# A four-layer graph network on one core: rows of indirect transfers, the place of the first keys, the last block of a scan, and the tables of the attention layer

## The chip, the cores and the metric

The kernel runs on one core of a Trainium2 chip. Its time is the time of one execution on the device in microseconds (us); a version is judged by the median over several executions. One further execution is recorded by the hardware profiler and gives the page and the trace that are read here. A core has five engines with a queue of instructions each: TensorE (PE, its weight loads are listed as PEld), VectorE (DVE), ScalarE (ACT), GpSimd (POOL) and SyncE (SP). SP, ACT and POOL also issue DMA transfers.

## The reference

There are 6250 nodes with 16 features each and 200000 edges sorted by their target node. Every layer gathers a row per edge by `src`, and reduces the rows of each target node `dst`.

```python
m = jnp.tanh(x[src] * edge_weight[:, None])                      # layer 0
agg0 = jax.ops.segment_sum(m, dst, num_segments=x.shape[0])
# layer 1, per edge a 16x16 matrix of messages and one of logits
e1 = (efeat @ W_msg + b_msg).reshape(E, 16, -1) * feat[src][:, :, None]
e2 = (efeat @ W_attn + b_attn).reshape(E, 16, -1) * feat[src][:, :, None]
seg_max = jax.ops.segment_max(e2, dst, num_segments=N)
ex = jnp.exp(e2 - seg_max[dst])
denom = jax.ops.segment_sum(ex, dst, num_segments=N)
agg1 = jax.ops.segment_sum(e1 * ex / denom[dst], dst, num_segments=N).sum(axis=1)
# layer 2
agg2 = jax.ops.segment_max(x[src] * timestamp, dst, num_segments=N) @ W.T + b
# layer 3, twice, relu between the passes
h = (1.0 + eps) * x + jax.ops.segment_sum(x[src], dst, num_segments=n)
h = jax.nn.relu(h @ wa + ba) @ wb + bb
# log_softmax at the end; after every layer
x = _layernorm(x + agg)
```

## The kernel before

**Layout.** 125 partitions hold 50 nodes each, and 1600 consecutive edges each. The edges of a partition are cut into 8 blocks of 200 columns (`NB`, `JB`).

**One scan over the edges.** `edge_scan` (L465) runs for layer 0 ("l0"), for layer 2 ("l2") and for both passes of layer 3 ("l3a", "l3b"). It works under an order written out by hand, and fills for each block a tile `xb` of 200 columns with the rows of the source nodes, from two sides. 120 columns (`NPE`) come from TensorE: ten batches of 12 columns (`BC`), three selects of 4 columns in each. A batch needs one-hot matrices, which DVE makes (L462) of keys loaded from a DRAM tensor `key_d` (L456, two batches ahead); a select is a row of matmuls (L491) of the one-hots with the node features split in three bfloat16 parts, then a DVE multiply that keeps what belongs to the column (L495) and a DVE sum (L500) into `xb`. The other 80 columns are gathered by POOL, one indirect DMA of 125 rows for a column (L97), all 80 issued at the start of a block; `xb` has two buffers. In the third batch of the next block `message` is applied to the whole block (layer 0: multiply by the edge weight L890 and tanh L891; layer 2: multiply; layer 3: nothing), and then 16 scans along the 200 columns, one for each feature (L513 for the maximum, L517 for the sum), go between the selects of that block. Their result goes to a DRAM table of rows. For the last block there is no next one: its message and its 16 scans come after its last select and its last gather.

**From rows to nodes.** After the scan the ends of partitions are carried over, and `at_nodes` (L587) gathers for each of the 50 node columns the row at which the node's edges end, 50 indirect DMAs of 128 rows (tile `an_y`). The 50 columns are taken in two chunks, `CHUNKS = ((0, 40), (40, NJ))`; for each chunk `finish` does the layer's matmuls, the layer normalisation, the store of the new node table (`into_table`) and the split in parts (`split_table`). The order of these two chunks on the engines is decided by the scheduler of the framework.

**The beginning.** `src` and `dst` are loaded, DVE checks whether the edges are sorted (`n_back`), and all engines branch on that (L232, the body sorts). Three large DRAM copies (`ew_d` twice and `ef_d`, 14.4 MB) are issued by ACT before the branch (L220), after a one-element copy `arrived` of `src`. The keys of the first block are made after the branch on DVE and PE (`keys_made`, `keys_turned`, `keys_kept`, up to tile `kT`), stored to `key_d` by SP (L274), and loaded by `edge_scan`. SP's queue after the branch is: the load of `ew` (L887, 800 KB), the store of `key_d`, three loads of keys.

**Beside layer 0.** `prelude` hands `edge_scan` a list of jobs by select number, which prepare layer 1: the search for the last edge of each node, with 51 gathers of 128 rows into `in_run` (`ends_gather`, L406); the list of attention chunks, written by 50 scatters of 128 rows (`chunks_put`, L744); and the edge table `edges_d`. On POOL the `in_run` gathers stand between the gathers of blocks 1 and 2, and the scatters between those of blocks 3 and 4. Tiles `run_i`, `ck_rows` and `ck_at` have 128 partitions, of which the last three are filled with constants.

**Layer 1.** `steps` (L990) makes 220 steps. Each ends with one store of 128 rows of 3 KB (L1083): sums of weights, weighted sums, and maxima, 256 numbers of each. Afterwards one gather `fx` (128 rows) and 50 gathers `r` (128 rows of 3 KB, five into a buffer, three buffers) fetch what the nodes need; ACT takes the logarithm and the exponential of the sums (L1233, L1234), DVE multiplies and sums (L1236, L1237), and the two chunks are finished as above. Of `r` only the first two thirds of a row are used.

Of the kernel before, what the change touches and what calls it, by code (L numbers as in the profile page):

```python
# [41 lines left out]
CHUNKS = ((0, 40), (40, NJ))  # L42
# [5 lines left out]
def tile_gnn_resnorm(ctx: ExitStack, tc: tile.TileContext, a: dict, out: bass.AP):  # L48
# [166 lines left out]
    arrived = consts.tile([1, 1], F32, name="arrived")  # L215
    with tc.manual_schedule():

        nc.scalar.copy(arrived, src[:1, :1])
        for to, of in given[2:]:
            nc.scalar.dma_start(to.rearrange("(p j) f -> p (j f)", p=80),  # L220
                                of.rearrange("(p j) f -> p (j f)", p=80))
    with tc.tile_pool(name="sort", bufs=1) as sp, tc.tile_pool(name="sortp", bufs=1, space=PSUM) as pp:
        back = sp.tile([P, J], F32, name="backwards")
        worst = sp.tile([P, 1], F32, name="worst")
        nc.vector.tensor_tensor(back, dst[:, 1:J + 1], dst[:, :J], op=OP.is_lt)
        nc.vector.tensor_reduce(worst, back, AX.X, OP.max)
        n_ps = pp.tile([1, 1], F32, name="n_ps")
        nc.tensor.matmul(n_ps, worst, ones, start=True, stop=True)
        n_back = sp.tile([1, 1], I32, name="n_back")
        nc.vector.tensor_copy(n_back, n_ps)  # L230
        unordered = nc.values_load(n_back, min_val=0, max_val=P)
        with tc.If(unordered > 0):  # L232
            sort_edges(sp, pp, dst)
            nc.sync.dma_start(src, src_d.rearrange("(p j) o -> p (j o)", j=J))
            load_dst(dst, dst_d.rearrange("e o -> (e o)"))

# [42 lines left out]
    with tc.tile_pool(name="keys0p", bufs=1, space=PSUM) as pp:  # L279
        keys_kept(kp, 0, keys_turned(lambda r, c: pp.tile([128, 512], F32, name="scratch")[:r, :c], keys_made(kp, 0)))  # L280
# [74 lines left out]
    def ends_begin(sp):  # L355
        e = Ends()
        e.runs = sp.tile([P, NR + 1], F32, name="runs")
        nc.vector.tensor_copy(e.runs[:, :NR], dst[:, 1:J + 1].rearrange("p (r k) -> p r k", k=RUN)[:, :, RUN - 1])
        nc.vector.tensor_copy(e.runs[:, NR:], rank[:P])
        edge = sp.tile([P, 2], F32, name="dst_edge")  # L360
        nc.vector.tensor_copy(edge[:, 0:1], dst[:, :1])
        nc.vector.tensor_scalar(edge[:, 1:2], rank[:P], float(P - 1), BIG, op0=OP.is_equal, op1=OP.mult)
        nc.vector.tensor_add(edge[:, 1:2], edge[:, 1:2], e.runs[:, NR - 1:NR])

        e.from_ = sp.tile([P, 2, NJ1], F32, name="from_edge")
        nc.vector.tensor_tensor(e.from_, edge.unsqueeze(2).to_broadcast([P, 2, NJ1]),
                                io[:P, :NJ1].unsqueeze(1).to_broadcast([P, 2, NJ1]), op=OP.subtract)
        nc.vector.tensor_scalar(e.from_, e.from_, 1.0, None, op0=OP.add)
        e.run = sp.tile([P, NJ1], F32, name="run")
        e.run_i = sp.tile([128, NJ1], I32, name="run_i")  # L370
        nc.vector.memset(e.run_i[96:], 0)
        e.inside, e.row_ps = {}, {}
        return e
# [18 lines left out]
    def ends_runs(sp, e, j0):  # L392
# [11 lines left out]
        nc.vector.tensor_copy(e.run_i[:P, here], e.run[:, here])  # L404

    def ends_gather(sp, e):  # L406
        e.in_run = sp.tile([128, NJ1, RUN], I32, name="in_run")
        for j in range(NJ1):
            gather(e.in_run[:, j, :], runs_d, e.run_i[:, j:j + 1])

    def ends_upto(sp, e, j0):
        here = slice(j0, j0 + 17)
        less = sp.tile([P, 17, RUN], BF16, name="less_in")
        nc.vector.tensor_tensor(less, e.in_run[:P, here], nodes[:, here].unsqueeze(2).to_broadcast([P, 17, RUN]),
                                op=OP.is_le)
        nc.vector.tensor_reduce(upto[:, here], less, AX.X, OP.add)
# [37 lines left out]
    def load_keys(ep, k, bufs=2):  # L454
        keys = ep.tile([P, BW], U16, name="keys", bufs=bufs)
        nc.sync.dma_start(keys, key_d[k * BC * P:k * BC * P + BW].partition_broadcast(P))  # L456
        return keys

# [6 lines left out]
    def edge_scan(tag, table, parts, F, message, pen, tmp, beside=None, first=None):  # L465
# [10 lines left out]
        with tc.tile_pool(name=f"es_{tag}", bufs=3) as ep, \  # L476
# [4 lines left out]
            NBT = NPE // BC  # L481
            batches = [(b, c) for b in range(NB) for c in range(NBT)]

# [18 lines left out]
            def scans(xb, b, prev):  # L502
# [3 lines left out]
                if prev is not None:  # L506
                    last = ep.tile([P, F], F32, name="last", bufs=2)
                    nc.vector.tensor_copy(last, prev[:, JB - 1, :])

                def one(f):  # L510
                    if is_max:
                        init = -BIG if last is None else last[:, f:f + 1]
                        nc.vector.tensor_tensor_scan(sc[:, :, f], pen[:, b * JB:(b + 1) * JB], xb[:, :, f],  # L513
                                                     init, op0=OP.add, op1=OP.max)
                    else:
                        init = 0.0 if last is None else last[:, f:f + 1]
                        nc.vector.tensor_tensor_scan(sc[:, :, f], keep[:, b * JB:(b + 1) * JB], xb[:, :, f],  # L517
                                                     init, op0=OP.mult, op1=OP.add)

                pieces = [lambda f=f: one(f) for f in range(F)]  # L520
                pieces.append(lambda: store(nc.sync, rows_v[:, b * JB:(b + 1) * JB, :], sc))
                return sc, pieces

            keys = [load_keys(ep, k) for k in range(0 if first is None else 1, 2)]
            ohs = one_hot(ep, keys.pop(0)) if first is None else first
            prev, todo, waiting = None, [], []
            for k, (b, c) in enumerate(batches):
# [10 lines left out]
                if c == 2 and waiting:  # L538
                    xw, bw = waiting.pop(0)
                    message(xw, bw)  # L540
                    prev, todo = scans(xw, bw, prev)
# [12 lines left out]
            for xw, bw in waiting:  # L554
                message(xw, bw)
                prev, todo = scans(xw, bw, prev)
                while todo:
                    todo.pop(0)()
# [150 lines left out]
    def chunks_set(tmp, num, stop, off_ps, all_ps):  # L709
# [16 lines left out]
        rows_all = tmp.tile([128, NJ, 4], F32, name="ck_rows")  # L726
        nc.vector.memset(rows_all[96:], 0.0)
        rows = rows_all[:P]
# [7 lines left out]
        at = tmp.tile([128, NJ], I32, name="ck_at")  # L736
        nc.vector.memset(at[96:], 128 * Q)
        nc.vector.tensor_copy(at[:P], first)
# [3 lines left out]
        return rows_all, at  # L742

    def chunks_put(rows_all, at):  # L744
        for j in range(NJ):
            nc.gpsimd.indirect_dma_start(
                out=chunk_d[j % NC], out_offset=bass.IndirectOffsetOnAxis(ap=at[:, j:j + 1], axis=0),
                in_=rows_all[:, j, :], in_offset=None, bounds_check=128 * Q - 1, oob_is_err=False)
# [138 lines left out]
    nc.sync.dma_start(ew, ew_d.rearrange("(p j) o -> p (j o)", j=J))  # L887

    def tanh_message(xb, b):
        nc.vector.tensor_mul(xb, xb, ew[:, b * JB:(b + 1) * JB].unsqueeze(2).to_broadcast([P, JB, D]))  # L890
        nc.scalar.activation(xb, xb, AF.Tanh)  # L891

    def prelude(kp):
# [65 lines left out]
        at(10, lambda: put(r=edge_rows_begin(now["rp"])))  # L959
        for i in range(J // WE):  # L960
            for step in range(4):
                at(16 + 3 * i + step, lambda i=i, step=step: edge_rows(now["r"], i * WE, step))
# [6 lines left out]
    rows, carry = edge_scan("l0", a["x"], parts, D, tanh_message, None, lp0, prelude(kp))  # L969
# [15 lines left out]
    rows1 = dram.tile([128 * Q, RW], F32, name="rows_l1")  # L985
    rows1_v = rows1.rearrange("(p t) c -> p t c", t=Q)
    l1o = ctx.enter_context(ExitStack())
    tail = l1o.enter_context(tc.tile_pool(name="l1o", bufs=1)).tile([128, RW], F32, name="tail")
    with tc.tile_pool(name="l1c", bufs=1) as cp:
        def steps(lo, hi, state, between=None):  # L990


            with tc.tile_pool(name=f"l1i{lo}", bufs=3) as ip, \
# [87 lines left out]
                def keep_state(t, ps, st):  # L1081
                    nc.scalar.copy(st[:, :2 * DD], ps)
                    nc.sync.dma_start(rows1_v[:, t, :], st)  # L1083
# [48 lines left out]
        nc.sync.dma_start(rows1_v[:, QS:, :], zero.unsqueeze(1).to_broadcast([128, Q - QS, RW]))  # L1132
# [7 lines left out]
    first = one_hot(fp, load_keys(fp, 0, 1), 1)  # L1140
# [4 lines left out]
    with tc.tile_pool(name="l1t", bufs=1) as lp, tc.tile_pool(name="l1tp", bufs=1, space=PSUM) as pp:  # L1145
# [49 lines left out]
        gather(fx, rows1, fix_row)  # L1195
# [28 lines left out]
        for j0, j1 in CHUNKS:  # L1224
            n = j1 - j0
            y = lp.tile([P, n, D], F32, name=f"y1_{j0}")
            for j in range(j0, j1, GN):
                r = lp.tile([128, GN, RW], F32, name="r", bufs=3)
                for i in range(GN):
                    gather(r[:, i, :], rows1, idx_row_all[:, j + i:j + i + 1])  # L1230
                v = r[:P, :, :2 * DD].rearrange("p j (i k o) -> p j i k o", k=2, o=D)
# [3 lines left out]
                for i in range(GN):  # L1235
                    nc.vector.tensor_mul(A[:, i], A[:, i], L[:, i])  # L1236
                    nc.vector.tensor_reduce(y[:, j - j0 + i, :], A[:, i].rearrange("p i o -> p o i"), AX.X, OP.add)  # L1237
            nc.vector.tensor_mul(y, y, own[:, j0:j1].unsqueeze(2).to_broadcast([P, n, D]))
# [46 lines left out]
    with tc.tile_pool(name="l2", bufs=1) as lp:  # L1285
# [5 lines left out]
        def scaled_message(xb, b):  # L1291
            nc.vector.tensor_mul(xb, xb, ew1[:, b * JB:(b + 1) * JB].unsqueeze(2).to_broadcast([P, JB, D]))

        rows, carry = edge_scan("l2", t2, parts, D, scaled_message, pen, lp, first=first)
        with tc.tile_pool(name="l2p", bufs=2, space=PSUM) as pp:
# [9 lines left out]
            at_nodes(lp, rows, carry, D, True, finish)  # L1305


    def gin(tag, table, parts, xt, F, ws, lp, then):
# [3 lines left out]
        rows, carried = edge_scan(tag, table, parts, F, lambda xb, b: None, None, lp, first=first)  # L1312
        with tc.tile_pool(name=f"{tag}p", bufs=2, space=PSUM) as pp:
# [21 lines left out]
            at_nodes(lp, rows, carried, F, False, finish)  # L1335
# [75 lines left out]
```

## Time and profile before

| what | value |
|---|---|
| median of 6 runs | 7623.91 us (7621.07 to 7626.5) |
| profiled execution | 7624.68 us |
| span of its profile | 7622.9 us |
| granted TensorE clock, mean | 0.957 of full speed |
| PE busy | 6794.4 us, 89% |
| DVE busy | 6744.3 us, 88% |
| POOL busy | 5861.1 us, 77% |
| ACT busy | 1903.4 us, 25% |

Times within the profile are counted from the start of its span. In a row of a timeline the columns are start, duration (of the whole run of `xN` instructions), engine, line, operation, output and inputs, and in brackets the idle time of the engine just before with what ended it. In a row of a group the columns are line, engine, operation, names and count, then busy time and mean duration in ns, then the idle time before them. Layer 0 takes the time up to about 1250 us, layer 1 up to 4324, layer 2 up to about 5440, the passes of layer 3 up to 6529 and to the end.

### The profile page before, as it was taken

To read this page: it belongs to the slowest core of one execution; us is meant where nothing else is said; L and a number is where in the kernel's file an instruction comes from. 1 tells how busy PE (TensorE), PEld (TensorE's weight loads), DVE (VectorE), ACT (ScalarE), POOL (GpSimd) and SP (SyncE) were. 2 spreads that over 40 slices of the span, in tenths; PEclk is the share of its full clock that TensorE was granted. 3 is DMA by queue.
4 is the path that set the end of the run, shared out by engine and by line. 5 is a ranking of instruction groups with operands and counts; after the bars stand their busy time and mean duration, and the time that the engine had idled before them with its cause. 6 is when DMAs were issued, how large, how long until landed. Compare 5 with 4: busy or idle time off the path is not lost. (4 is left out here: it accounts for less than half of the span.)

```text
span 7622.9 us, 133196 instructions
## 1 busy us (share of the span) xinstructions
PE 6794.4 (89%) x55586; PEld 5220.7 (68%) x55586; DVE 6744.3 (88%) x7804; ACT 1903.4 (25%) x3200; POOL 5861.1 (77%) x4906
## 2 busy tenths in 40 slices
PE   5889894999999999999999499998599997899995
PEld 5888894444444444444444399998599997799994
DVE  6999995999999999999999789997588886688985
ACT  0122110555555555555555300000000000000000
POOL 5787886777777777777777588887688887788886
PEclk9999997999999999999999799999799998899997
DMA  4344542122222212222221422222122222122221
GB/s 128 93 115 100 124 95 76 48 53 50 53 50 52 53 50 53 50 53 51 51 53 48 134 45 45 56 46 45 34 47 54 47 54 45 30 53 47 56 45 33
DMA packets 288130, 460.36 MB, mean 60 GB/s; under 512 B 134733, under 2 KB 188133, under 8 KB 283216
## 3 DMA queue, kind: packets, MB, share of 16 engines
q1 hardware_dynamic: 121136, 331.29, 12.8%
q0 software_dynamic: 166032, 105.92, 11.4%
q10 hardware_dynamic: 336, 14.40, 0.6%
q8 instruction: 442, 7.24, 0.4%
q14 instruction: 184, 1.51, 0.1%
HBM read 256.64 MB, written 206.15 MB: 61 GB/s over the span
## 5 line engine op out<-in xcount | busy, mean ns | idle before, releaser
L491 PE MATMUL all_ps<-parts,oh 125*128 125x208 bf16 (+1 forms) x46080 | 4006.8, 251 | 205.8 <-DVE kept L495 78.3
L491 PEld LDWEIGHTS <-oh 125*128 125x128 bf16 x46080 | 3987.4, 99 | 224.8 <-issue 99.3
L97 POOL DMA_INDIRECT hg<-table_x,g x1760 | 2062.2, 1172 | 544.0 <-issue 539.1
L97 POOL DMA_INDIRECT xb<-table_x,src x1280 | 1614.1, 1261 | 434.2 <-issue 414.5
L1077 PE MATMUL la<-e,ident 128*128 128x512 f32 x3520 | 1561.6, 597 | 4.5 <-DVE e L1064 3.8
L500 DVE TENSOR_REDUCE xb<-kept 125x64 f32<-125x832 f32 x960 | 1509.6, 1572 | 33.0
L495 DVE TENSOR_TENSOR kept<-all_ps,place 125x832 f32<-125x832 f32 x960 | 974.4, 1015 | 354.0 <-PE all_ps L491 345.5
L1077 PEld LDWEIGHTS la<-e,ident 128*128 128x128 f32 x3520 | 653.1, 191 | 744.1 <-issue 737.4
L97 POOL DMA_INDIRECT xb<-in_x,src x640 | 834.5, 1304 | 250.8 <-issue 193.9
L1029 DVE TENSOR_TENSOR e<-mm,hg 128x1024 f32<-128x1024 f32 x880 | 1013.5, 1208 | 3.4 <-DMA hg<-table_x,g 3.3
L97 POOL DMA_INDIRECT xb<-table_l3b,src x640 | 796.4, 1244 | 211.4 <-issue 211.4
L1024 PE MATMUL mm<-w_h,eT 98*128 98x512 bf16 x1760 | 668.3, 380 | 236.6 <-DVE e L1029 167.6
L462 DVE TENSOR_SCALAR oh<-keys,mykey 125x1504 bf16<-125x1504 uint16 x1272 | 786.6, 678 | 72.9 <-DMA keys<-key_d 72.9
L1041 ACT ACTIVATE e<-e,epen 128x256 f32<-128x256 f32 x1760 | 797.3, 501 | 113.8 <-DVE e L1029 112.0
L1057 ACT ACTIVATE e<-e 128x1024 f32<-128x1024 f32 x440 | 465.1, 1057 | 1001.7 <-DVE e L1055 984.7
L1025 PE MATMUL mm<-w_l,eT 98*128 98x512 bf16 x1760 | 669.7, 381 | 0.0
L1025 PEld LDWEIGHTS <-eT 98*128 98x128 bf16 x1760 | 169.7, 96 | 636.6 <-issue 532.2
L1055 DVE TENSOR_TENSOR e<-e,st 128x1024 f32<-128x1024 f32 x440 | 519.2, 1221 | 7.7
L1064 DVE TENSOR_TENSOR e<-e 128x1024 f32<-128x1024 f32 x440 | 515.6, 1209 | 0.0
L1024 PEld LDWEIGHTS <-eT 98*128 98x128 bf16 x1760 | 170.9, 97 | 238.5 <-issue 57.1
L449 ACT ACTIVATE ln_s<-ln_s,eps_t 125x40 f32<-125x40 f32 (+1 forms) x8 | 2.4, 315 | 1181.7 <-DVE ln_s L448 1181.7
L97 POOL DMA_INDIRECT g<-edges_d,eidx x220 | 208.0, 946 | 91.8 <-PE la L1078 60.6
(366 smaller groups left out, 3388.1 us busy)
## 6 DMA issues: line engine op xcount, KB each, us to landing
keys<-key_d SPq DMA_DIRECT2D x318, 367.2 KB
rows_l<-st SPq DMA_DIRECT2D x220, 384.0 KB
edges_d<-er_t SPq DMA_DIRECT2D x64, 546.9 KB
hg<-table_x,g POOLq DMA_INDIRECT x1760
rows_l<-sc SPq DMA_DIRECT2D x16, 1400.0 KB
xb<-table_x,src POOLq DMA_INDIRECT x1280
ef_d<-in_edge_attr ACTq DMA_DIRECT2D x1, 12500.0 KB
er_ef<-ef_d SPq DMA_DIRECT2D x64, 175.0 KB
```

Of the source, the lines that this page charges most:

```text
L97: nc.gpsimd.indirect_dma_start(out=dst_ap, out_offset=None, in_=table, in_offset=bass.IndirectOffsetOnAxis(ap=idx, axis=0))
L462: nc.vector.tensor_scalar(oh[:, g, :], keys, mykey[:, g:g + 1], None, op0=OP.is_equal)
L491: nc.tensor.matmul(o, oh[:, g, (c + i) * P:(c + i) * P + 128], parts[:, q, a0:a0 + n, :].rearrange("p a f -> p (a f)"), start=(g == 0 and ...
L495: nc.vector.tensor_tensor(kept.rearrange("p (h i) a f -> p h (i a) f", i=2), all_ps[:P, :, :2 * W].rearrange("p h (i f) -> p h i f", f=F), ...
L500: nc.vector.tensor_reduce(xb[:, j:j + SG, :], kept.rearrange("p i a f -> p i f a"), AX.X, OP.add)
L1024: nc.tensor.matmul(ps[:, i, :], eT[:, s + i, :], w_h, start=True, stop=False)
L1025: nc.tensor.matmul(ps[:, i, :], eT[:, s + i, :], w_l, start=False, stop=True)
L1029: nc.vector.tensor_tensor(e[:, s:s + 2, :].rearrange("p s (i x) -> p (s i) x", x=2 * D), ps.rearrange("p s (i x) -> p (s i) x", x=2 * D), ...
L1041: nc.scalar.activation(part(e, 0)[:, k], part(e, 0)[:, k], AF.Identity, bias=epen[:, t, k:k + 1])
L1055: nc.vector.tensor_tensor(sc, sc, top.rearrange("p (i o) -> p i o", o=D).unsqueeze(1).to_broadcast([128, 4, D, D]), op=OP.subtract)
L1064: nc.vector.tensor_tensor(part(e, 1)[:, s:s + 4], part(e, 1)[:, s:s + 4], part(e, 0)[:, s:s + 4], op=OP.mult)
L1077: nc.tensor.matmul(ps, ident, e[:, s, :], start=(s == 0), stop=False)
```

## The change

- `in_run`, `run_i`, `ck_rows` and `ck_at` have 125 partitions; the 51 gathers and the 50 scatters move 125 rows. Three small memsets go, one of them for the constants of `run_i`, two for those of the scatters.
- The keys of the first block are made, stored and loaded ahead of the branch (`keys_first`), in the two tiles that layer 0's first two batches use; the branch's body makes them again. `arrived` now copies an element of the first keys tile, so that ACT issues the three large copies after that tile has landed. The copies are written with `p=1600` in place of `p=80`; the instructions that come of it have the same shapes.
- The load of `ew` becomes a job of layer 0 at select 20, split in 112 and 13 rows. The jobs that begin the edge rows move from 10 to 14 and from 16 to 19.
- The last block of every scan is worked in three parts: columns 0 to 72 after the sixth batch, beside the last selects; 72 to 120 after the last select; 120 to 200, the gathered columns, at the end. Message and scans are done by part. The store of the rows is one as before.
- `CHUNKS` is ((0, 35), (35, NJ)), and `at_nodes` in layers 2 and 3 is under an order by hand: everything of the first chunk, then everything of the second.
- The rows of layer 1 go to two DRAM tables, `rows_l1` with 2 KB rows (sums) and `top_l1` with 1 KB rows (maxima), by two stores in each step. `fx` is fetched by two gathers; the `r` gathers fetch 2 KB rows into four buffers, in groups of five and, at the end of each chunk, of three and two.

```diff
-CHUNKS = ((0, 40), (40, NJ))
+CHUNKS = ((0, 35), (35, NJ))
...
+        keys0 = keys_first([None, None])
+        arrived = consts.tile([1, 1], F32, name="arrived")
+        with tc.manual_schedule():
+
+            nc.scalar.copy(arrived, keys0[0][:1, :1])
+            for to, of in given[2:]:
+                nc.scalar.dma_start(to.rearrange("(p j) f -> p (j f)", p=1600),
+                                    of.rearrange("(p j) f -> p (j f)", p=1600))
+        with tc.If(unordered > 0):
...
+            keys_first(keys0)
...
-        e.in_run = sp.tile([128, NJ1, RUN], I32, name="in_run")
+        e.in_run = sp.tile([P, NJ1, RUN], I32, name="in_run")
...
+            CE = NBT - 4
...
+                if b == NB - 1 and c == CE:
+
+                    assert not todo
+                    message(xb, b, 0, CE * BC)
+                    sc, last = scans(b, prev)
+                    todo = pieces(xb, b, sc, last, 0, CE * BC)
...
-            for xw, bw in waiting:
-                message(xw, bw)
-                prev, todo = scans(xw, bw, prev)
-                while todo:
-                    todo.pop(0)()
+            for lo, hi in ((CE * BC, NPE), (NPE, JB)):
+                message(xb, b, lo, hi)
+                for do in pieces(xb, b, sc, last, lo, hi):
+                    do()
+            keep_rows(sc, b)
+            prev = sc
...
-        rows_all = tmp.tile([128, NJ, 4], F32, name="ck_rows")
-        nc.vector.memset(rows_all[96:], 0.0)
-        rows = rows_all[:P]
+        rows = tmp.tile([P, NJ, 4], F32, name="ck_rows")
...
-                    nc.sync.dma_start(rows1_v[:, t, :], st)
+                    nc.sync.dma_start(rows1_v[0][:, t, :], st[:, :2 * DD])
+                    nc.sync.dma_start(rows1_v[1][:, t, :], st[:, 2 * DD:])
...
-        gather(fx, rows1, fix_row)
+        gather(fx[:, :2 * DD], rows1, fix_row)
+        gather(fx[:, 2 * DD:], top1, fix_row)
...
-            for j in range(j0, j1, GN):
-                r = lp.tile([128, GN, RW], F32, name="r", bufs=3)
-                for i in range(GN):
+            j = j0
+            for m in [GN] * (n // GN - 1) + [GN - 2, 2]:
+                r = lp.tile([128, GN, 2 * DD], F32, name="r", bufs=4)
+                for i in range(m):
                     gather(r[:, i, :], rows1, idx_row_all[:, j + i:j + i + 1])
...
-            at_nodes(lp, rows, carried, F, False, finish)
+            with tc.manual_schedule():
+                at_nodes(lp, rows, carried, F, False, finish)
```

## The prediction

> **What bounds the kernel now.** I read the busy time by stage first, then the page's POOL groups, the durations of single POOL instructions, the waits of SP's queue, and the timelines of the places that the change touches. The windows are the stages: layer 0, layer 1, its end, layer 2, and the two passes of layer 3. Columns: window, its length, busy time of PE, PEld, DVE, ACT, POOL with the count of instructions, clock, DMA share, GB/s.
>
> ```profile
> 50.00:1250.00 1200.00, 1047.17 (x11644) 1029.28 (x11644) 1112.58 (x1557) 196.14 (x264) 938.51 (x745) 0.95 0.40 97
> 1250.00:4230.00 2980.00, 2726.15 (x9251) 1193.96 (x9251) 2865.14 (x3133) 1638.22 (x2866) 2320.47 (x2032) 0.98 0.21 53
> 4230.00:4324.00 94.00, 8.53 (x27) 4.17 (x27) 67.89 (x160) 57.53 (x51) 44.99 (x46) 0.52 0.65 212
> 4324.00:5440.00 1116.00, 1008.11 (x11614) 1003.08 (x11612) 915.68 (x984) 0.63 (x2) 865.28 (x692) 0.95 0.21 46
> 5440.00:6529.00 1089.00, 1002.82 (x11526) 995.24 (x11524) 882.10 (x966) 1.81 (x3) 844.97 (x690) 0.95 0.23 47
> ```
>
> In layer 0 POOL is the limit though its busy share is not the highest: 0.30 us of issue follows each of 745 instructions, so it is occupied for 938.5 + 223.5 = 1162 us. From its first row gather (59.87) to its last (1220.1) it has no gap. In the later passes PE (1003 to 1008 of about 1100 us) sets the pace. Now the price of one POOL instruction (minimum/median/maximum ns), and what POOL and SP waited for:
>
> ```profile
> L97 POOL DMA_INDIRECT xb<-in_x,src x640: 1205/1209/4522, 59.9 to 1218.9; - x160
> L97 POOL DMA_INDIRECT in_run<-runs_d,run_i x51: 940/944/1860, 314.9 to 378.9; - x51
> L746 POOL DMA_INDIRECT chunk_d<-ck_rows,ck_at x50: 971/972/1355, 639.2 to 703.6; - x50
> L97 POOL DMA_INDIRECT xb<-in_x,src x640 | 834.5, 1304 | 250.8 <-issue 193.9 <-DMA key_d<-kT 56.0 <-DVE w_am L635 0.3
> SPq L232 <- SPq L232: 45.0, 4, 38.6
> ```
>
> ```profile
> 11.03 1.23 ACTq L220 DMA_DIRECT2D ew_d<-in_edge_weight  x2
> 12.30 0.60 ACTq L220 DMA_DIRECT2D ef_d<-in_edge_attr  x1
> 59.27 0.32 SPq L274 DMA_DIRECT2D key_d<-kT  x1
> 59.87 1.39 POOL L97 DMA_INDIRECT xb<-in_x,src  x1 [55.98 <-DMA key_d<-kT]
> 74.36 4.14 DVE L462 TENSOR_SCALAR oh<-keys,mykey 125x1504 bf16<-125x1504 uint16 x6 [45.52 <-DMA keys<-key_d]
> ```
>
> The xb gathers have 125 rows and take 1.209 us; in_run and chunk_d, like every other gather here, have 128 rows and take 0.944 and 0.972. And SP sits 45.0 us at the branch L232: it leaves at 58.44, when the copies that ACT issued from 11.03 on have landed (their last packet ends at 58.09). POOL's first gather follows 1.43 us later; the kT that the page names had long been there (28.84). Last, three lines of the final tail:
>
> ```profile
> 7521.77 8.52 DVE L517 TENSOR_TENSOR_SCAN sc<-keep,last,xb 125x200 f32<-125x200 f32 x16 [3.97 <-issue]
> 7602.03 0.33 DVE L602 TENSOR_TENSOR an_y<-an_y,carried 125x160 f32<-125x160 f32 x1 [7.52 <-DMA an_y<-rows_l3b,idx_end]
> 7603.05 0.48 DVE L1276 TENSOR_TENSOR tn_o<-tn_ps,row_L_gnn_b2b 125x320 f32<-125x320 f32 x1
> ```
>
> Sixteen scans wait for the last gather; later DVE idles 7.52 us on the second chunk's gathers while the first chunk's L1276, ready, stands behind them in DVE's order.
>
> **The first keys ahead of the branch, the copies behind them.** In the changed kernel's instruction order the branch still waits for every hardware DMA queue, so the copies, now issued after the first keys load, decide again. n_back ends at 12.50; key_df to kT took 22.06 to 28.84 = 6.78 us, so kT ends at 19.3 and SP issues key_d by 19.6 (0.32). A small store followed by a dependent load took 2.3 us (table_x store issued to 4321.69, gather at 4324.00), so keys are issued at 22.2. They land in 4.6 to 6.0 us (1319.86 to 1324.44, 4322.06 to 4328.05): 27.5. The 0.19 us arrived copy follows, and the copies, the same three transfers, need their 47.06 us (11.03 to 58.09): 74.8. SP leaves 0.35 us later, POOL starts at 76.5 instead of 59.87. **+16.6 us on POOL** (14 to 20, by the landings). DVE's one-hots start near 76 rather than 74.36: 2 us, covered by POOL, which is the limit. SP's own order puts key_d and two keys loads ahead of the branch, nothing late waits behind them. The ew load, 0.8 MB ahead of key_d at 58.85, moves into select 20: ew is first read in the second block, over 100 us later, so nothing. Starting the edge rows four selects later is hidden by the blocks too, as are three small memsets that go.
>
> **Loads and scatters of 125 rows.** 51 + 50 POOL instructions go from 128 to 125 rows. The nearest row with 125 rows costs 1.209 - 0.944 = 0.265 us more: 101 x 0.265 = **+26.8 us**. Bounds: 0, if rows are not what makes xb dear; +34, by xb's mean period in layer 0 ((1220.1 - 59.9 - 64.0 - 64.4)/640 = 1.61 us, against 64.0/51 = 1.25 and 64.4/50 = 1.29). I take 26.8: hg gathers the same 64-byte rows with 128 rows at 0.945, so neither the width nor the table explains xb. Both groups lie in POOL's unbroken run. What is late next: block 4's gathers end at 833.7 and block 5's third batch, which needs them, starts some 20 us later; 43 us of delay stops DVE there, and PE with it, for about 23 us. POOL doesn't wait for them (block 6's buffer is free well before), so this adds nothing to POOL's end.
>
> The Trainium skill, DMA: Bandwidth & Descriptors, section Why a DMA increments its semaphore by 16 and not by 1, says that a transfer uses the largest number of engines up to 16 that divides its outer dimension, so 125 rows get 5 and 128 rows 16. It speaks against this part, but of the transfer and not of POOL's time. By the row the sum has 26.8 more; by that rule alone only landings move, which have tens of us to spare here, and it has 0.
>
> **The last block in three parts.** Per layer, what follows the last landing shrinks from 200 to 80 columns. Scans cost 0.533 (200 wide) and 0.406 (125 wide): 0.0017 a column, 0.33 for 80, 16 x 0.33 = 5.3 instead of 8.5. The multiply (3.49) and tanh (2.87) go by columns to 1.4 and 1.15. Layer 0: 3.49 + 2.9 + 8.55 becomes 1.4 + 1.2 + 5.3, **-7.0**; layer 2: -2.1 - 3.2 = **-5.3**; the two passes of layer 3: **-3.2** each. The first part (72 columns) goes beside the last selects, where DVE waits about 1.48 us for PE in each of 12 and two one-hots (2.35 each) fall away, about 22 us for some 6; uncovered, 6 us. The middle part lasts 16 x 0.28 = 4.4 us, about POOL's lag at the ends of layer 3.
>
> **Chunks of 35 and 15, ordered by hand.** At the end of layer 0 some ten DVE steps go from 160 to 240 wide (0.32 and 0.82 for 160 and 640: +0.08 each): **+0.8**. In layer 2 the first chunk's chain takes about 16 us by its own instructions, and now ends within the second's 15 gathers (15 x 1.25 = 18.7). Left after the last landing is the second chunk alone, about 13.5 us where 5420.22 to 5438.19 was 18.0: **-4.5**. Layer 3a likewise, 11 for 14.9: **-4**. In 3b the first chunk, with softmax and logs, takes about 23 us, so the second starts 4.4 late, and its table loads come twice: **+1**. Bounds -6 to +3 for each.
>
> **Two tables in layer 1.** 220 more SP issues of about 0.3 us, in steps of 13.5 us where DVE (2865 of 2980) is the limit: nothing; uncovered, 66 us, but DVE doesn't wait for these stores. At its end POOL needed 74.6 us (4224.19 to 4298.81) for 50 r gathers of 1.245 = 62.3: 12.3 lost waiting for three buffers and 3 KB rows. With four buffers and 2 KB rows that goes, less a second fx gather of 1.25: **-11**. Other bound: **+5**, if ScalarE holds the end (12 groups instead of 10, each with two 1.28 us table loads).
>
> Sum: 16.6 + 26.8 - 7.0 - 5.3 - 3.2 - 3.2 + 0.8 - 4.5 - 4 + 1 - 11 = +7.0. The profiled execution took 7624.68 (span 7622.9 and 1.8 around it), 0.8 above the median of 7623.91; so 7631.7, and 7631 as a median. About 0.2%, or 15 us, is what a measurement of this kernel can tell from no change: I forecast none.
>
> **Rivals.** *Rows are not the price*: for it, only that no 128-row gather stands in xb's place; against it, hg. Sum without 26.8: 7604. *The branch lets go without the copies*, so the part doesn't do what I say: POOL starts near 30, 46 us sooner than forecast, 7585; against it, the 45.0 us row. *Slower: ScalarE holds the end of layer 1*: its loads and activations for 12 groups are 30.7 + 25.4 = 56.1 us, with fx's about 61, as much as POOL's 62.3. Then +5 for -11: 7647. It decides once that end gives back under 3 us. For it, ACT is already busy for 57.5 of 94 us there; against it, POOL's idle is mostly put down to DVE and DMA.
>
> **How the numbers follow.** Forecast 0.45 (7631, alone 7617 to 7645: same 0.30, slower 0.12, faster 0.03); rows not the price 0.15 (faster 0.11, same 0.04); free branch 0.08 (faster); ScalarE 0.22 (slower 0.20, same 0.02); anything else 0.10 (0.03 faster, 0.02 same, 0.05 slower). Together faster 0.25, same 0.38, slower 0.37. The range 7597 to 7656 leaves out the free branch and the far ends.
>
> **What would show it.** POOL's first gather near 76.5 and its last of layer 0 near 1263; in_run and chunk_d at 1.21 to 1.24 us; scans of 80 columns near 0.33; the span from first r gather to layer 2's first xb gather down from 99.8 to about 89; 13 to 14 us from the second chunk's landing to layer 3a's first gather. Wrong it is made by an early POOL start, cheap 125-row instructions, or first chunks that don't end in time.

## The result and the profile after

The changed kernel takes 7644.55 us (median of 16 runs, 7640.25 to 7646.65) beside 7624.47 us before in the same set: a ratio of 1.0026, 95% interval 1.0019 to 1.0032. It is slower by 20 us. The forecast was 7631 us with no change that can be told; the time lies in the range of 7597 to 7656, but what came is the case that had a chance of 0.37. The profiled execution has a span of 7646.4 us, 23.5 us more than before.

The price of one POOL instruction in the changed kernel (minimum/median/maximum ns), and SP's wait at the branch:

```profile
L97 POOL DMA_INDIRECT xb<-in_x,src x640: 1205/1210/4524, 75.9 to 1266.0; - x160
L97 POOL DMA_INDIRECT in_run<-runs_d,run_i x51: 1205/1210/2350, 332.7 to 410.7; - x51
L769 POOL DMA_INDIRECT chunk_d<-ck_rows,ck_at x50: 1186/1195/3088, 672.4 to 750.6; - x50
SPq L289 <- SPq L289: 52.6, 6, 39.0
```

in_run went from 0.944 to 1.210 us, the price of xb's 125 rows, and chunk_d from 0.972 to 1.195. POOL's last gather of layer 0 starts at 1266.0 instead of 1218.9. The beginning, from the timeline of the changed kernel:

```profile
19.04 0.28 DVE L251 CAST kT<-scratch 120x125 uint16<-120x125 f32 x1
21.31 54.38 SPq L262 DMA_DIRECT2D keys<-key_d  x3
27.46 1.23 ACTq L287 DMA_DIRECT2D ew_d<-in_edge_weight  x2
28.73 0.60 ACTq L287 DMA_DIRECT2D ef_d<-in_edge_attr  x1
74.90 4.63 DVE L469 TENSOR_SCALAR oh<-keys,mykey 125x1504 bf16<-125x1504 uint16 x8 [55.57 <-SPq L289]
75.86 1.56 POOL L97 DMA_INDIRECT xb<-in_x,src  x1 [71.97 <-SPq L289]
```

The first keys tile is there before 27.46, when the copies that wait for it are issued. DVE's one-hots (74.90) and POOL's first gather (75.86) wait for SP's branch all the same, and SP waits for these copies, which were issued 16.4 us later than before and whose last packet ends at 74.33. The final tail:

```profile
7547.85 3.46 DVE L533 TENSOR_TENSOR_SCAN sc<-keep,sc,xb 125x48 f32<-125x48 f32 x16
7551.48 4.52 DVE L533 TENSOR_TENSOR_SCAN sc<-keep,sc,xb 125x80 f32<-125x80 f32 x16 [0.17 <-DVE sc L533]
7608.43 0.74 DVE L628 TENSOR_TENSOR an_y<-an_y,carried 125x560 f32<-125x560 f32 x1 [45.03 <-DMA an_y<-rows_l3b,idx_end]
7617.52 0.49 DVE L1306 TENSOR_TENSOR tn_o<-tn_ps,row_L_gnn_b2b 125x320 f32<-125x320 f32 x1 [4.40 <-PE tn_ps L1305]
7629.31 0.40 DVE L628 TENSOR_TENSOR an_y<-an_y,carried 125x240 f32<-125x240 f32 x1
```

After the last landing come 4.52 us of scans instead of 8.52, and the first chunk's L1306 no longer stands behind the second chunk's L628, which now waits for its turn only. What didn't come as forecast is the end of layer 1:

```profile
4259.99 0.27 SPq L262 DMA_DIRECT2D keys<-key_d  x1
4260.55 0.27 SPq L1319 DMA_DIRECT2D ew<-ew_d  x1
4262.88 1.32 POOL L97 DMA_INDIRECT r<-rows_l,idx_row  x1 [0.30 <-issue]
4279.37 1.28 ACT L1262 ACT_TABLE_LOAD   x1 [9.28 <-DMA r<-rows_l,idx_row]
```

From the first r gather to ACT's first work on the first group pass 16.5 us. Ahead of the r gathers SP has issued two loads for layer 2 (keys, 367 KB, and the edge weights, 781 KB, that is 800,000 bytes). In the kernel before, the same place reads:

```profile
4224.19 0.95 POOL L97 DMA_INDIRECT r<-rows_l,idx_row  x1 [0.30 <-issue]
4230.33 0.27 SPq L1289 DMA_DIRECT2D ew<-ew_d  x1
4236.00 1.28 ACT L1233 ACT_TABLE_LOAD   x1 [2.84 <-DMA r<-rows_l,idx_row]
```

There ACT begins 11.8 us after the first r gather. The edge weights were issued behind the first five r gathers, and the keys long before, at 1319.86.

How the delay of the changed kernel builds up, from the starts and ends of the same instructions in the two traces (differences are taken before rounding):

| step | before, us | after, us | difference | forecast |
|---|---|---|---|---|
| POOL's first gather | 59.87 | 75.86 | +16.0 | +16.6 |
| from there to the last gather's end of layer 0 | 1160.2 | 1191.4 | +31.1 | +26.8 |
| from there to the last scan of layer 0 | 16.8 | 9.1 | -7.8 | -7.0 |
| from there to the first r gather of layer 1 | 2987.2 | 2986.6 | -0.7 | +0.8 |
| from there to layer 2's first xb gather | 99.8 | 105.3 | +5.5 | -11 |
| layer 2, to the last gather's end | 1010.3 | 1012.6 | +2.2 | 0 |
| its scans, after that | 13.6 | 7.4 | -6.2 | -5.3 |
| from its last scan to layer 3a's first xb gather | 90.2 | 85.6 | -4.7 | -4.5 |
| layer 3a: gathers; scans; to 3b | 993.3; 10.3; 87.0 | 991.9; 7.3; 84.1 | -1.4; -3.0; -2.8 | 0; -3.2; -4 |
| layer 3b: gathers; scans; to the end | 991.2; 10.4; 92.6 | 992.7; 6.1; 90.4 | +1.5; -4.3; -2.2 | 0; -3.2; +1 |
| sum | | | +23.5 | +7.0 |

### The profile page after: what moved, and what is told of

The parts are those of the page before. It is cut to its first block, busy times and chain, and to the rows that moved or that the text cites. A ratio compares the mean times of both kernels' runs of the same rounds, so it can differ in the third digit from the quotient of the medians.

```text
span 7646.4 us, 133776 instructions
## 1 busy us (share of the span) xinstructions
PE 6796.8 (89%) x55586; PEld 5220.5 (68%) x55586; DVE 6761.0 (88%) x7933; ACT 1915.4 (25%) x3214; POOL 5899.0 (77%) x4907
## 5 line engine op out<-in xcount | busy, mean ns | idle before, releaser
L1054 DVE TENSOR_TENSOR e<-mm,hg 128x1024 f32<-128x1024 f32 x880 | 1013.0, 1208 | 11.1 <-DMA hg<-table_x,g 10.5
```

The source lines that it names most:

```text
L1054: nc.vector.tensor_tensor(e[:, s:s + 2, :].rearrange("p s (i x) -> p (s i) x", x=2 * D), ps.rearrange("p s (i x) -> p (s i) x", x=2 * D), ...
```

## The experiments

Ratios are to the kernel before, run in turn on the same chip; its median was 7624 to 7631 us in the sets below, so versions of different sets are compared by ratio or by stretches of the trace.

**128 rows again in in_run and chunk_d.** The changed kernel with

```diff
-        e.run_i = sp.tile([P, NJ1], I32, name="run_i")
+        e.run_i = sp.tile([128, NJ1], I32, name="run_i")
+        nc.vector.memset(e.run_i[96:], 0)
...
-        e.in_run = sp.tile([P, NJ1, RUN], I32, name="in_run")
+        e.in_run = sp.tile([128, NJ1, RUN], I32, name="in_run")
...
```

and the same for ck_rows and ck_at.

> The changed kernel with in_run, run_i, ck_rows and ck_at back at 128 rows, all else as changed. Theory, the row price and POOL's run set layer 0: in_run and chunk_d go back to 0.94 and 0.97 us, POOL's last gather of layer 0 ends 31 us earlier (near 1236), and the whole kernel is 31 us faster, near 7614. Rival, the dearer rows were mostly covered and other things make layer 0 longer: under 10 us faster.

7629.15 us, ratio 0.9997 (0.9987 to 1.0006), where the changed kernel had 1.0026: the loss is gone.

```profile
L97 POOL DMA_INDIRECT in_run<-runs_d,run_i x51: 943/947/1290, 331.3 to 394.7; - x51
```

The price is back at 0.947, and POOL's last gather of layer 0 ends at 1242.0, 25.2 us earlier than in the changed kernel. That is less than the 31 expected. The two groups' own stretches give back 26.6 us (80.4 to 64.4 and 79.5 to 68.9); chunk_d's 68.9 stays 3.5 us above the 65.4 before, though its median is back at 0.974. The xb gathers of the eight blocks take 2.1 us more than in the changed kernel; single blocks differ by up to some 2 us between runs.

**One number in the kernel before: xb gathers of 128 rows.**

```diff
-GP = 125
+GP = 128
```

> The kernel before with one number changed: the xb gathers take 128 rows (three more that nobody reads). Theory, the count of rows is what makes xb dear: its gathers fall from 1.21 to 0.94 us, POOL stops being the limit of layer 0 and no longer lags PE at the ends of layers 2 and 3 (19 us in layer 2): 20 to 30 us faster, near 0.9965 of the time before. Rival, xb's tile or place in the block makes it dear: 1.21 stays, no change.

7579.31 us, ratio 0.9942 (0.9925 to 0.9958): 47 us faster, more than expected.

```profile
L97 POOL DMA_INDIRECT xb<-table_x,src x1280: 938/944/3556, 4309.1 to 6316.1; - x183
L97 POOL DMA_INDIRECT xb<-in_x,src x640: 938/944/3558, 60.1 to 1140.0; - x160
L97 POOL DMA_INDIRECT xb<-table_l3b,src x640: 940/944/1278, 6486.3 to 7401.1; - x160
```

Same tables, same tile, three rows more: 0.944 instead of 1.209. The rival is out: the count of rows sets the price. Only these two counts were run, and why 125 rows hold POOL longer than 128 no run shows. POOL's last gather of layer 0 ends at 1141.0 instead of 1220.1, of layer 2 at 5231.4 instead of 5334.3, and its lag at the end of the layers is gone. By the two traces the gain is 14.3 us in layer 0, 20.0 in layer 2 (the 19 us of POOL's lag that were expected), 7.5 and 3.4 in the two passes of layer 3. In layer 0 the selects themselves, from the first to the last, take 1124.9 instead of 1136.1 us. The expectation had named layer 0 and the ends of layers 2 and 3; together they were worth more than it gave them.

**Copies early, first keys still ahead of the branch.** The changed kernel with

```diff
-            nc.scalar.copy(arrived, keys0[0][:1, :1])
+        nc.scalar.copy(arrived, src[:1, :1])
```

and this block moved back to where src is loaded.

> The changed kernel with the three large copies issued as early as before (behind src, not behind the first keys); the first keys stay ahead of the branch. Theory, the copies hold the branch and with it POOL: SP leaves near 58.5, POOL starts near 60 instead of 75.9, layer 0 ends 16 us earlier, the kernel near 7629. Rival, the keys loads now share the DMA engines with the copies and hold DVE's one-hots longer than the branch did: POOL starts early all the same, but DVE's first select stays at 83 or later and the gain is under 8 us.

Ratio 1.0017 (1.0008 to 1.0027) beside 1.0026. POOL starts at 65.99, 9.9 us earlier and not 16; the end of layer 0 moves by the same 9.8. The wait of SP's queue tells where the other 6 went:

```profile
SPq L262 <- DMA key_d<-kT: 27.4, 1, 27.4
```

The store of kT is issued at 19.44, but its 29 KB land only at about 47, while the copies are under way. Of the 734 KB of the two keys loads that follow it, 702 KB move between 57.5 and 64.3, when the copies are nearly or wholly done (their last packet ends at 58.88), and the branch opens after that, at 65. So the copies did hold the branch of the changed kernel, as the theory has it; issued first, they push the keys behind them, and the keys hold it. POOL still starts 6 us later than in the kernel before (59.87). DVE's first select sum starts at 72.5 instead of 83.3, against the rival's condition. What that alone is worth this run can't tell, since POOL starts earlier by nearly as much; POOL still sets the end, its last gather ending 24.7 us after the last select sum (1257.4 and 1232.7). The ratio gains 0.0009, some 7 us, and the two intervals overlap.

**The edge weights of layer 2 away from the r gathers.** The changed kernel with

```diff
-        nc.sync.dma_start(ew1, ew1_d.rearrange("(p j) o -> p (j o)", j=J))
+        ew1_load = {20: [lambda: store(nc.sync, ew1, ew1_d.rearrange("(p j) o -> p (j o)", j=J))]}
...
-        rows, carry = edge_scan("l2", t2, parts, D, scaled_message, pen, lp, first=first)
+        rows, carry = edge_scan("l2", t2, parts, D, scaled_message, pen, lp, ew1_load, first=first)
```

and the keys tile of layer 2 in one buffer.

> The changed kernel with the edge weights of layer 2 loaded at select 20 of layer 2, and the first keys tile of layer 2 in a pool with one buffer as before, so that neither load is issued just ahead of the r gathers. Theory, these 1.1 MB ahead in the DMA queues make the first r group land late: the stretch from the first r gather to layer 2's first xb gather (105.3 us) becomes 95 to 100, the kernel 5 to 10 us faster. Rival, ScalarE's 12 groups hold that end: the first group lands earlier but the stretch shrinks by less than 2.

The stretch from the first r gather to layer 2's first xb gather is 99.0 us instead of 105.3. The keys load stayed where it was (4264.73 in this trace), and ACT, DVE and POOL do the same instructions in the same order over this stretch, so the 6.3 us belong to the edge weights alone. Other traces repeat it: with the weights ahead of the r gathers the stretch takes 104.4 to 106.5 us in five other runs of this section, whose edits lie elsewhere or change the groups; with the weights moved it takes 99.0, 98.9 and, with groups of five, 97.5 in the three runs at the end of this section.

```profile
4276.90 1.28 ACT L1262 ACT_TABLE_LOAD   x1 [2.23 <-DMA r<-rows_l,idx_row]
...
4298.33 0.43 DVE L1217 TENSOR_TENSOR fx<-fx 128x256 f32<-128x256 f32 x1 [5.13 <-ACT fx L1216]
...
4304.53 1.24 POOL L97 DMA_INDIRECT r<-rows_l,idx_row  x1 [4.96 <-issue]
```

ACT now starts 9.3 us after the first r gather (4267.62), not 16.5. The whole shows nothing of it (ratio 1.0022, 1.0012 to 1.0032, beside 1.0026): the gain is about as large as the intervals. And 99.0 is only where the kernel before was (99.8), not the 89 that the forecast had: POOL still waits 4.96 us in the middle, now with four buffers. The trace puts this wait down to issue, that is to nothing it shows. What fits is the buffer of the second group, which the sixth takes over: DVE's last sum of the second group ends at 4303.8, 0.7 us before the gather. These sums stood behind L1217 in DVE's order, and DVE had idled 5.13 us there for ACT's work on `fx`.

**Groups of five only.** `[GN] * (n // GN - 1) + [GN - 2, 2]` becomes `[GN] * (n // GN)`.

> The changed kernel with all r groups of five (ten groups instead of twelve). Theory, ScalarE's table loads hold the end of layer 1: four table loads of 1.28 us fall away and the stretch from the first r gather to layer 2's first xb gather (105.3 us) shrinks by about 5. Rival, late landings hold it: less than 2, or the last group of five costs what the loads save.

Ratio 1.0027 (1.0017 to 1.0037); the stretch is 104.4 instead of 105.3. Two groups less are worth 0.9 us here, and 1.4 in the last run of this section (98.9 to 97.5): the table loads of the added groups are not what makes this end long.

**No logarithm in the r groups.** The version with the edge weights moved, without

```diff
-                nc.scalar.activation(L, L, AF.Ln)
```

> The run with the two loads moved away from the r gathers, and in the r groups the logarithm left out (only the exponential is taken, so the attention layer's result is not the reference's; its own table stays loaded from group to group). Theory, ScalarE with its two table loads a group still holds the end of layer 1: the stretch from the first r gather to layer 2's first xb gather shrinks from 99.0 to 92 or less. Rival, POOL's gathers and DVE's sums hold it: 97 or more.

This kernel was executed once (7635.89 us). The stretch is 92.4 us instead of 99.0, r gathers 69.3 of it instead of 71.6, the rest 23.1 instead of 27.4. This is just above the bound that was set for ScalarE's theory, and far from the 97 of its rival. With the logarithms 25 of 28 table loads go, and the waits of the middle shrink:

```profile
4290.92 0.47 DVE L1217 TENSOR_TENSOR fx<-fx 128x256 f32<-128x256 f32 x1 [1.03 <-ACT fx L1216]
```

No r gather waits longer than 0.33 us now. So ScalarE's logarithms and table loads hold up to 6.6 us of this end. It is not quite one change: the scheduler also put some of DVE's instructions in another order, and no run tells the two apart. POOL's gathers take 69.3 even so, 7 us above 50 x 1.245: the 50 instructions themselves take 54.3 us, where their usual 0.947 would give 47.4. What makes them longer was not tested.

**The chunks without the order by hand.**

```diff
-            with tc.manual_schedule():
-                at_nodes(lp, rows, carry, D, True, finish)
+            at_nodes(lp, rows, carry, D, True, finish)
```

and the same in layer 3.

> The changed kernel with the order by hand taken off the two chunks in layers 2 and 3 (the chunks stay 35 and 15). Theory, the hand order is what shortens these tails: layer 2 loses 5 us, 3a 3 us, 3b 2 us, in all 8 to 10 slower than the changed kernel. Rival, the smaller second chunk's earlier first landing does it: under 3.

Ratio 1.0030 (1.0019 to 1.0042). The stretches after the scans grow by 2.6 us in layer 2 (85.6 to 88.2), by hardly anything in 3a (84.1 to 84.5), by 1.4 in 3b (90.4 to 91.8): about 4 in all, half of what was expected. The ratios (1.0030 and 1.0026) can't tell so little. The line that shows the order is the first chunk's L463 in layer 2, here 3.3 us behind the second chunk's first step:

```profile
5461.42 0.41 DVE L626 TENSOR_TENSOR an_y<-an_y,carried 125x240 f32<-125x240 f32 x1 [9.99 <-DMA an_y<-rows_l,idx_end]
5464.70 0.74 DVE L463 TENSOR_TENSOR x<-tn_o,ln_s 125x560 f32<-125x560 f32 x1
```

With the order by hand, in the changed kernel, it stands before the second chunk's first step:

```profile
5453.54 0.80 DVE L463 TENSOR_TENSOR x<-tn_o,ln_s 125x560 f32<-125x560 f32 x1
5461.40 0.41 DVE L626 TENSOR_TENSOR an_y<-an_y,carried 125x240 f32<-125x240 f32 x1 [3.45 <-issue]
```

The rest of these three gains (-4.7, -2.8, -2.2) is left for the cut at 35, as the last block in one piece (below) doesn't change these stretches (85.8, 84.2, 90.5); no run changed the cut alone.

**The last block in one piece.**

```diff
-            for lo, hi in ((CE * BC, NPE), (NPE, JB)):
-                message(xb, b, lo, hi)
-                for do in pieces(xb, b, sc, last, lo, hi):
-                    do()
+            message(xb, b, 0, JB)
+            sc, last = scans(b, prev)
+            for do in pieces(xb, b, sc, last, 0, JB):
+                do()
```

and without the first part in the loop.

> The changed kernel with the last block of every scan in one piece as before. Theory, the three parts are what shortened the four tails (7.8, 6.2, 3.0 and 4.3 us against before): about 21 us slower than the changed kernel, 1.0053 of before. Rival, the tails shortened for other reasons (POOL's later end in layer 0, order): under 10.

Ratio 1.0048 (1.0031 to 1.0065): about 17 us slower than the changed kernel by the ratios, whose intervals are wide, and 12.5 by the two spans. From the last gather's end to the last scan the four tails are 16.8, 13.7, 10.3 and 10.5 us, where the three parts leave 9.1, 7.4, 7.3 and 6.1: the 21 us are there. But the gathers of the last block are quicker without the parts: 126.3 instead of 128.6 us in layer 0, 125.6 instead of 128.8 in layer 2, where POOL ends last. The kernel before, in one piece too, has 126.1 and 125.6; six more runs of the changed kernel's family with three parts have 128.2 to 129.1 and 127.1 to 128.9. So the first part's DVE work beside the last selects is not free; it slows POOL by 2 to 3 us in layer 0 and 1.5 to 3 in layer 2. Some 4 us more of POOL's earlier end in layer 0 arise in blocks that the edit doesn't touch, and stay unexplained.

**The parts that pay, together.** The changed kernel with 128 rows in all indirect transfers (in_run, chunk_d, xb) and the edge weights of layer 2 moved:

> The changed kernel with 128 rows in every indirect transfer (in_run, chunk_d and xb) and the two loads of layer 2 away from the r gathers. Theory, with the row price gone everywhere layer 0 is set by PE again and the three-part last block and the hand order keep their gains: 40 to 50 us faster than before, near 0.994. Rival, PE and the one-hots leave no room and only the 31 us of the rows come back: 0.9985.

7566.32 us, ratio 0.9922 (0.9906 to 0.9939): 60 us faster, more than expected. Beside the kernel before with 128 rows in xb its span is 9.4 us shorter and its ratio 0.0020 lower (some 15 us, with overlapping intervals): about that much the other parts, with the weights moved, are worth once the price of rows is gone. The same with the copies issued early:

> As the run with 128 rows everywhere and the loads moved, and the three large copies issued early again, behind src. Theory, DVE's one-hots, now what layer 0 waits for, start 9 to 11 us earlier (72.5 for the first select sum as in the run with early copies, where it was 83.3): 10 us faster than that run. Rival, layer 0 is still held by POOL: under 3.

7554.49 us, ratio 0.9907 (0.9891 to 0.9924). Layer 0 ends at 1207.1 instead of 1217.5, 10.4 us earlier, as the theory has it. DVE's first select sum moved by 10.5 us (83.4 to 72.9) and POOL's start by 10.7, but POOL's last gather now ends 67 us before the last select sum (1127.7 and 1194.5), so it is the selects' earlier start that counts. And with groups of five:

> 128 rows in every indirect transfer, loads of layer 2 moved, copies issued early, and all r groups of five. Theory, four table loads less at the end of layer 1 are worth 1 us at most: near 0.9905 of before, as the same without the last edit. Rival, ScalarE holds that end now that the rest is quicker: 5 us, 0.990.

7553.71 us, ratio 0.9908 (0.9891 to 0.9924): the same time. So the rival has no support. This family beats both kernels, the one before by about 71 us.

## Why the prediction was right and where it was wrong

- **Layer 0** was right in mechanism and size. The branch held POOL until 75.86 (76.5 said) because the copies had been put behind the keys; the run with early copies confirms the hold, for POOL then starts 9.9 us earlier. The 125 rows cost what xb's row said: 1.210 and 1.195 us for 1.209. The prediction's other reading of the rows, by which only landings move and the sum has 0, is out. Of the +31.1, 26.8 was forecast; the two groups' own stretches grew by 29.5 (65.0 to 80.4 and 65.4 to 79.5): by the medians alone it would be 24.7, the rest is single instructions that took longer. Some 2.5 us more are the last block's gathers, slowed by the first part of the scans.
- **The rival that rows are not the price** had 0.15 and fell with one number changed.
- **The rival of a free branch** had 0.08 and fell with SP's 52.6 us row.
- **The three-part last block**: -7.8, -6.2, -3.0 and -4.3 for -7.0, -5.3, -3.2 and -3.2. The scans of 80 and 48 columns took 0.283 and 0.216 us (4.52 and 3.46 for 16), where the line through 200 and 125 columns had given 0.33 and 0.28. The first part, which "goes beside the last selects", was costed at nothing; it cost POOL 1.5 to 3 us in each of layers 0 and 2, so the parts gained 12 to 17 us and not the 21 of the four tails.
- **The chunks**: -4.7 and -2.8 for -4.5 and -4. In 3b the forecast was +1 and it was -2.2: the first chunk's chain let the second start at 7629.31, 2.2 us after the end of the second's last gather (7627.12), and not 4.4 us after its landing.
- **The step that failed is "Two tables in layer 1 ... that goes, less a second fx gather of 1.25: -11".** It was +5.5, and the miss of 16.5 us is the whole difference between forecast (+7.0) and trace (+23.5). That the other errors cancel, +31.1 for +26.8 among them, is luck. (By the medians the miss is 13.5 us, 7644.55 for 7631; the profiled execution was one of the longer ones.) Two things were overlooked. I did not look at what SP issues ahead of the r gathers in the changed order: the edge weights of layer 2 had come forward, and cost 6.3 us. And the 12.3 us that POOL lost were put down to three buffers and 3 KB rows, while a buffer comes free only when DVE has summed its group, and DVE waits for ScalarE: with the weights out of the way, four buffers and 2 KB rows leave the end at 99.0 us, 0.8 better than before. Leaving out the logarithms with their table loads takes up to 6.6 more. The last 3.4 us of the 89 that were forecast, beside r gathers that took longer than their usual 0.947, stay unexplained.
- **The slower rival** named this place and a size of +5 and a total of 7647, and both came, but the number by luck: 6.3 us of it are the edge weights, which it did not name. Its reason holds in part. Without the weights the end gives back 0.8 us, under the 3 that it set, and ScalarE's logarithms and table loads hold up to 6.6; the two added groups, from which it took its +5, are worth 0.9 to 1.4.

## What to carry to other kernels

Price an indirect transfer with its count of rows in mind, and not by its bytes alone: here three rows less cost 0.265 us in every instruction, and three rows more that nobody reads were the largest gain of the study. When large copies hold a join, small work that is moved ahead of it may only change what waits: put before the copies it delayed them, put behind them its own small store took 27 us to land. A saving on an engine that isn't the limit (the earlier one-hots) should be kept in mind, for it can count once the limit is gone. When instructions near a hand-over are rearranged, list what each DMA queue now issues first, not only what the engines do.

## What the runs showed of the hardware

- An indirect DMA held POOL 0.944 us with 128 rows and 1.209 with 125 (medians), whether it gathered 64 bytes a row (xb) or 160 (in_run: 0.944 and 1.210); a scatter of 16 bytes a row 0.972 and 1.195. With 2 KB and 3 KB rows of 128 it was 0.947 and 0.946: from 64 bytes to 3 KB a row POOL's time did not change.
- In layer 0 147 of 640 xb gathers of 125 rows took over 0.1 us longer than their median of 1.209; with 128 rows 61 of 640 took over 0.1 us longer than 0.944.
- A 29 KB store on SP's queue landed 27 us after its issue while 14.4 MB of copies from ACT's queue were under way. In the changed kernel, with these copies issued later, the keys load that depends on it was issued 2.0 us after it (19.35 and 21.31).
